# Moving one PSUM copy ahead of two normalising passes in a hand-ordered graph kernel

## The chip, the cores and the metric

The kernel runs on one core of a Trainium2 chip. The metric is the device time of one execution in microseconds, as the median of several runs. The engines are called PE (matrix engine; PEld is its loading of weights), DVE (vector), ACT (scalar, activations), POOL (GpSimd) and SP (which issues most DMAs).

## The reference

The input is a batch of 128 graphs of 128 nodes with 512 features, in fp32. Two layers follow each other, each on a normalised copy of the features (layernorm, then ReLU) with a residual connection.

```python
# layer 0: attention with 8 heads, scores multiplied by twice the adjacency
h = relu(layernorm(x))
q, k, v = h @ Wq.T + bq, h @ Wk.T + bk, h @ Wv.T + bv
scores = (q @ k.T) / sqrt(64) * (adj + adj)
x = x + (softmax(scores) @ v) @ Wo.T + bo
# layer 1: graph attention
h = relu(layernorm(x))
Wh = h @ W
e = leaky_relu(Wh @ a[:512] + (Wh @ a[512:]).T, 0.2)
att = softmax(where(adj > 0.5, e, -9e15), axis=1)   # over the rows
x = x + elu(att @ Wh)
```

## The kernel before

The kernel treats the batch as 64 pairs p of two graphs. The work on a pair is cut into small named steps (functions that issue a few instructions), and three lists give the order in which steps of different pairs are issued: HEAD at the start, ORDER for each round of the middle, TAIL at the end. Each engine then executes its own instructions in the order of issue. In ORDER a step is written `name:lag`, and round p issues it for the pair p - lag. So a round works on several pairs at once: in round p the scores of layer 0 belong to pair p, the contexts to pair p - 1, the normalising of layer 1 to pair p - 2 and the gather of layer 1 to pair p - 3.

The steps that matter here:

```python
    # all PSUM tiles come from one pool of eight
    ps1 = ctx.enter_context(tc.tile_pool(name="ps1", bufs=8, space=bass.MemoryType.PSUM))

    def row_stats(src, name, soon=False):                 # cut
        def stats(i):                                     # st0, st1: DVE
            nc.vector.bn_stats(st, src[:, i, :])
            nc.vector.bn_aggr(mv[:, i, :], st)
        def power():                                      # pw: POOL, 1/sqrt(var + eps)
            if not soon:
                nc.gpsimd.tensor_scalar_add(mv[:, :, 1], mv[:, :, 1], EPS)
            nc.gpsimd.tensor_tensor(mv[:, :, 1], mv[:, :, 1], mhalf.to_broadcast([P, 2]), OP.pow)

    def centre1(p):                                       # nm: DVE
        nc.vector.scalar_tensor_tensor(nmr, mv[:, :, 0], -1.0, mv[:, :, 1], op0=OP.mult, op1=OP.mult)

    def hidden1(p, i):                                    # h20, h21: ACT, normalising of batch i
        nc.scalar.activation(
            h1s[p][0][:, i, :], xs[p][:, i, :], AF.Relu, bias=nmr[:, i : i + 1], scale=mv[:, i, 1:2]
        )

    def dot1(p, i, k):                                    # d00 ... d11: DVE, reads what h20, h21 wrote
        ...

    def gather1(p, i):                                    # g0, g1: PE, the gather of batch i
        pg = ps1.tile([P, C, S], F32, name="pg", tag="ps1")
        for c in range(C):
            nc.tensor.matmul(pg[:, c, :], h1s[p][0][:, i, c * P : (c + 1) * P], wts[p][:, i, :], start=True, stop=True)
        pgs[p, i] = pg

    def keep_gathered(p, i):                              # ge0, ge1: ACT, copy of the gathered rows
        if p not in gTs:
            gTs[p] = work.tile([P, 7, 2, S], F32, name="gT")
        nc.scalar.copy(rows_of(gTs[p], i), pgs.pop((p, i)))

    def scores(b):                                        # sca, scb: PE, two PSUM tiles each
        ...
    def weigh(b, k):                                      # ata0, ata1, atb0, atb1: DVE, scores times adjacency
        ...                                               # then mxa (DVE), exa0-3 (ACT), fla (DVE)
    def context(b):                                       # pca, pcb: PE, one PSUM tile each
        pc = ps1.tile([P, C, S], F32, name="pc", tag="ps1")
        for j in range(C):
            for s in range(2):
                nc.tensor.matmul(pc[s * D : (s + 1) * D, j, :], vs[b // G][...], aT[:, :, s * C + j, :], start=True, stop=True)
    def keep_context(b):                                  # pea, peb: ACT
        nc.scalar.copy(rows_of(cxT, b % 2), pcs.pop(b))
```

The other names of ORDER that the text speaks of: U1 to U11 are the products for q, k and v (acc_a, acc_b, acc_c), F their copies by ACT, A their additions by DVE; o and w are the output products of the two layers (row_a, row_c). The first line of ORDER, which opens a round, is before

```
        U1:0 fa:4 ge0:3 pw:2 hs1:1 fb:4 g1:3 nm:2 lT:0 so:4 sca:0 h20:2 scb:0 h21:2 ata0:0 ge1:3 ata1:0 pca:1 mxa:0
        pcb:1 pea:1 d00:2 F1:0 U11:1 exa1:0 ...          # cut
```

The middle has the rounds p = 3 to 59. Odd and even rounds differ in which of the U products they issue.

Of the kernel before, what the change touches and what calls it, by code (L numbers as in the profile page):

```python
# [24 lines left out]
def kernel(  # L25
# [548 lines left out]
    def listed(text, mark):  # L574
# [24 lines left out]
        od6@1 od5@1 m1@0 e1@0 U7@2 A9@2 sw@0 st1@1 g0@0 F7@2 st0@1 F10@2 Ww3@0 A2@2 hd1@2  # L599
    """  # L600
    ORDER = """
        U1:0 fa:4 ge0:3 pw:2 hs1:1 fb:4 g1:3 nm:2 lT:0 so:4 sca:0 h20:2 scb:0 h21:2 ata0:0 ge1:3 ata1:0 pca:1 mxa:0
        pcb:1 pea:1 d00:2 F1:0 U11:1 exa1:0 A6:1 A8:1 U2:0 exa0:0 d10:2 exa3:0 t0:0 px:2 exa2:0 gs0:3 rca0:0 w0:3 pd:2
        A11:1 A10:8 A1:8 nma1:0 rca1:0 w1:3 gs1:3 t1:0 nma2:0 gs2:3 o0:1 s0:0 zc0:3 nma0:0 lx:1 wd1:3 U3:0 nma3:0 hs3:1
        d01:2 fla:0 o1:1 F3:0 peb:1 w2:3 atb0:0 bla:0 atb1:0 w3:3 zc2:3 mxb:0 F2:0 la:-1 w4:3 pv:2 gs3:3 lt:2 U5:0 zc4:3
# [223 lines left out]
```

## Time and profile before

| | |
|---|---|
| time, median of 3 runs | 2364.43 us (2360.34 to 2364.67) |
| span of the profiled run | 2362.5 us |
| mean granted TensorE clock | 0.997 |
| copy gT, ACT, 128 x 512, 128 times | 576 ns median |
| normalising pass h, ACT, 128 x 512, 128 times | 812 ns median |
| DMA traffic | 314.06 MB, mean 133 GB/s |

A busy line of the profile has an engine, its busy time in us, its share of the span and its instructions. A line of the timeline has the start in us from the start of the span, the length of the merged group, engine, line of the kernel, operation, output and inputs with shapes, the number of instructions, and in brackets how long the engine had been idle and what released it. A wait that is put down to one engine is the one of several that ended last.

### The profile page before, as it was taken

The numbers are of one execution on the slowest core, as the hardware profiler recorded it, in microseconds if no ns is written. First come the engines' busy times: TensorE is split into PE (matmuls) and PEld (weight loads), VectorE is DVE, ScalarE is ACT, GpSimd is POOL, SyncE is SP. The second block draws the span as 40 slices with busy tenths as digits, with TensorE's granted clock in tenths as the row PEclk, the third lists the DMA queues.
The fourth block names the chain that finished last, engine by engine and source line by source line (L and its number), as shares of the span: only waits on it lengthen the run. The fifth ranks groups of instructions, "written<-read, shape, count | busy, mean of one in ns | idle before, by whom it ended". The sixth has DMA issues, their size and how long they took to land.

```text
span 2362.5 us, 41114 instructions
## 1 busy us (share of the span) xinstructions
PE 2337.6 (99%) x14184; PEld 2066.2 (87%) x14184; DVE 2002.0 (85%) x4113; ACT 1458.1 (62%) x4815; POOL 256.9 (11%) x320
## 2 busy tenths in 40 slices
PE   9999999999999999999999999999999999999998
PEld 8888888888888888888888888888888888888886
DVE  5888888888888888888888888888888888888888
ACT  2656666666566665666666666656666565666775
POOL 1101101111101011011110111110101101110000
PEclk8999999999999999999999999999999999999999
DMA  4444353454444544444535345444454443443332
GB/s 156 140 115 148 123 152 114 127 157 127 140 131 125 149 131 135 139 114 143 148 124 152 117 123 159 125 142 126 130 147 132 134 139 113 145 147 119 117 119 94
DMA packets 267353, 314.06 MB, mean 133 GB/s; under 512 B 24201, under 2 KB 192137, under 8 KB 267145
## 3 DMA queue, kind: packets, MB, share of 16 engines
q1 hardware_dynamic: 263112, 311.31, 43.5%
q8 instruction: 112, 1.84, 0.3%
q0 software_dynamic: 1920, 0.13, 0.2%
q14 instruction: 97, 0.79, 0.1%
q10 hardware_dynamic: 2112, 0.01, 0.1%
HBM read 210.51 MB, written 100.85 MB: 132 GB/s over the span
## 4 chain that ended last, share of the span: by engine, by line
PE 89%; DVE 4%; POOL 3%; ACT 3%; issue 1%; DMA 0%; POOLq 0%; ACTq 0%; SPq 0%; DVEq 0%
PE acc_a L258 26%; PE row_a L299 23%; PE acc_c L258 12%; PE row_c L299 8%; PE acc_b L258 7%; PE pc L388 5%; PE sc L320 3%; PE pg L481 3%; POOL mv L173 2%; ACT h L418 2%; DVE st L165 2%; POOL mv L172 1%; DVE x L402 1%; DVE v L279 1%; ACT gT L487 1%
## 5 line engine op out<-in xcount | busy, mean ns | idle before, releaser
L339 ACT ACTIVATE at<-at,nmx 128x128 f32<-128x128 f32 x1024 | 396.2, 391 | 18.0 <-DVE nmx L334 17.9
L299 PE MATMUL row_a<-wo,cxT 128*128 128x256 f32 x1280 | 328.5, 379 | 0.3 <-DVE cxT L153 0.3
L348 ACT ACTIVATE at<-at,rs 128x128 f32<-128x128 f32 x1024 | 323.8, 392 | 4.3 <-DVE rs L343 4.1
L299 PE MATMUL row_a<-w,gT 128*128 128x256 f32 x1280 | 319.4, 380 | 2.9 <-DVE z L499 1.7
L172 POOL TENSOR_SCALAR mv<-mv 128x2 f32<-128x2 f32 x124 | 79.1, 638 | 2033.0 <-DVE mv L166 2010.8
L299 PEld LDWEIGHTS row_a<-w,gT 128*128 128x128 f32 x1280 | 242.3, 190 | 37.9 <-DVE z L499 2.6
L299 PEld LDWEIGHTS row_a<-wo,cxT 128*128 128x128 f32 x1280 | 242.6, 190 | 34.3 <-DVE cxT L153 0.6
L402 DVE TENSOR_TENSOR x<-row_a,x 128x256 f32<-128x256 f32 x320 | 135.2, 422 | 146.6 <-PE row_a L299 143.8
L495 ACT COPY z<-row_a 128x256 f32<-128x256 f32 x256 | 94.6, 369 | 210.2 <-PE row_a L299 210.0
L275 ACT ACTIVATE kT<-acc_a,bk 128x256 f32<-128x256 f32 x256 | 106.7, 467 | 178.4 <-PE acc_a L258 175.2
L327 DVE SCALAR_TENSOR_TENSOR at<-sc,adj 128x512 f32<-128x512 f32 x256 | 165.1, 686 | 42.2 <-PE sc L320 39.8
L339 ACT ACTIVATION_READ_ACCUMULATOR at<-at,nmx 128x1 f32 x1024 | 194.4, 190 | 0.0
L418 ACT ACTIVATE h<-x,nmr,mv 128x512 f32<-128x512 f32 x128 | 97.5, 807 | 151.2 <-DVE nmr L412 148.9
L165 DVE BATCH_NORM_STATS2 st<-x 128x6 f32<-128x512 f32 x256 | 176.3, 689 | 7.4 <-DMA x<-in_x 5.0
L275 ACT ACTIVATE qT<-acc_a,bq 128x256 f32<-128x256 f32 x256 | 106.3, 467 | 123.1 <-PE acc_a L258 123.1
L425 DVE SCALAR_TENSOR_TENSOR junk<-h,u 128x512 f32<-128x512 f32 x256 | 173.5, 678 | 0.6
L355 DVE STREAM_TRANSPOSE tr<-at 128x1024 f32<-128x1024 f32 x128 | 158.9, 1241 | 7.0 <-PE pc L388 2.7
L334 DVE TENSOR_REDUCE nmx<-at 128x8 f32<-128x1024 f32 x128 | 156.2, 1220 | 4.3
L481 PEld LDWEIGHTS pg<-w,h 128*128 128x128 f32 x1024 | 133.3, 192 | 6.6 <-ACT z L495 0.2
L388 PE MATMUL pc<-aT,v 128*64 128x128 f32 x2048 | 127.6, 277 | 11.1 <-ACT gT L487 11.0
L173 POOL TENSOR_TENSOR mv<-mv,mhalf 128x2 f32<-128x2 f32 x128 | 131.0, 1024 | 30.9 <-DVE mv L168 20.6
L481 PE MATMUL pg<-w,h 128*128 128x128 f32 x1024 | 134.1, 275 | 0.0
(130 smaller groups left out, 4868.0 us busy)
## 6 DMA issues: line engine op xcount, KB each, us to landing
blocks<-tr SPq DMA_DIRECT2D x128, 512.0 KB, 6.5
aT<-blocks SPq DMA_DIRECT2D x512, 128.0 KB, 2.9
x<-in_x SPq DMA_DIRECT2D x123, 512.0 KB, 5.1
out<-x SPq DMA_DIRECT2D x63, 512.0 KB, 4.1
hA<-in_xT SPq DMA_DIRECT2D x120, 256.0 KB, 3.6
mr<-rows SPq DMA_DIRECT2D x60, 256.0 KB, 4.1
adj<-in_adj SPq DMA_DIRECT2D x64, 128.0 KB, 4.1
adjT<-in_adjT SPq DMA_DIRECT2D x64, 128.0 KB, 3.7
```

Source lines behind the costliest of these rows:

```text
L165: nc.vector.bn_stats(st, src[:, i, :])
L173: nc.gpsimd.tensor_tensor(mv[:, :, 1], mv[:, :, 1], mhalf.to_broadcast([P, 2]), OP.pow)
L258: nc.tensor.matmul(acc[:, m, :], lhsT, rhs, start=fresh and m == 0 and c == 0, stop=c == 1, skip_group_check=True)
L275: nc.scalar.activation(dst(t, f)[:, m, :], a[:, m, :], AF.Identity, bias=bias[:, j : j + 1])
L299: nc.tensor.matmul(acc, left[:, la, c, :], w[:, wb, c, :], start=n in (0, 3) and c == 0, stop=c == 1, skip_group_check=True)
L327: nc.vector.scalar_tensor_tensor(ats[b][0][:, k * C : (k + 1) * C, :], scs[b][k], QSCALE, adjs[p][:, i : i + 1, :].to_broadcast([P, C, S]) ...
L339: nc.scalar.activation(at[:, j, :], at[:, j, :], AF.Exp, bias=nmx[:, j : j + 1], accum_out=sums[:, j : j + 1])
L348: nc.scalar.activation(at[:, j, :], at[:, j, :], AF.Copy, scale=rs[:, j : j + 1])
L355: nc.vector.transpose(trs[b], at.rearrange("p h (j k) -> p j h k", k=Q))
L388: nc.tensor.matmul(pc[s * D : (s + 1) * D, j, :], vs[b // G][:, b % G, head * D : (head + 1) * D], aT[:, :, s * C + j, :], start=True, sto ...
L425: nc.vector.scalar_tensor_tensor(junk, h2[:, i, :], 1.0, u_sb[:, k, :], op0=OP.mult, op1=OP.mult, accum_out=ws[:, i, 1:2] if k else src_sb ...
L481: nc.tensor.matmul(pg[:, c, :], h1s[p][0][:, i, c * P : (c + 1) * P], wts[p][:, i, :], start=True, stop=True)
```

## The change

In ORDER the step ge1 moves from behind h21 and ata0 to the place ahead of h20. ACT thus copies the second gathered tile of pair p - 3 before it normalises the two batches of pair p - 2. Nothing else moves; HEAD and TAIL stay as they are. It is meant to free the PSUM tile of the second gather without waiting for the statistics that the normalising needs.

```diff
     ORDER = """
-        U1:0 fa:4 ge0:3 pw:2 hs1:1 fb:4 g1:3 nm:2 lT:0 so:4 sca:0 h20:2 scb:0 h21:2 ata0:0 ge1:3 ata1:0 pca:1 mxa:0
+        U1:0 fa:4 ge0:3 pw:2 hs1:1 fb:4 g1:3 nm:2 lT:0 so:4 sca:0 ge1:3 h20:2 scb:0 h21:2 ata0:0 ata1:0 pca:1 mxa:0
         pcb:1 pea:1 d00:2 F1:0 U11:1 exa1:0 A6:1 A8:1 U2:0 exa0:0 d10:2 exa3:0 t0:0 px:2 exa2:0 gs0:3 rca0:0 w0:3 pd:2
```

## The prediction

> **What bounds the kernel now.** I read the shares of busy time first, then who waited for whom, then the chain of waits around one instance of the longest wait of the matrix engine (PE), and last the timeline of two neighbouring rounds of the middle.
>
> ```profile
> PE 2337.6 (99%) x14184; PEld 2066.2 (87%) x14184; DVE 2002.0 (85%) x4113; ACT 1458.1 (62%) x4815; POOL 256.9 (11%) x320
> ```
>
> PE is busy for 2337.6 of 2362.5 us. Only about 25 us are idle, and that is nearly all that a change of order alone could bring back. From the view of waits:
>
> ```profile
> ACT h L418 <- DVE nmr L412: 148.9, 60, 3.1
> ...
> PEld pc L388 <- ACT gT L487: 16.6, 29, 0.6
> ...
> PE pc L388 <- ACT gT L487: 11.0, 28, 0.4
> ```
>
> The columns are total us, times, longest. ACT waits some 2.5 us per round before it normalises (148.9 / 60), which costs nothing by itself. But PE waits in turn for a copy that ACT makes after it: the context products (pc) wait for the copy of gathered rows (gT), 0.4 us, 28 times, 11.0 us. No other wait of PE exceeds 2.7 us in the whole run. The chain of waits from 1080 to 1090 us says how that wait comes about (start, us, what):
>
> ```profile
> 1082.37 1.02 POOL mv L172
> ...
> 1083.47 1.76 POOL mv L173
> ...
> 1085.25 0.17 DVE nmr L412
> ...
> 1085.51 1.52 ACT h L418 x2
> 1087.03 0.48 ACT gT L487
> 1087.51 0.04 issue
> 1087.55 1.97 PE pc L388 x32
> ```
>
> The statistics go through two slow POOL operations, then nmr on DVE, then two normalising passes on ACT (h20, h21), and only then comes the copy ge1, though it needs nothing of all that. PE stands behind it. The timeline of an odd round:
>
> ```profile
> 1084.12 1.05 PE L481 MATMUL pg<-w,h 128*128 128x128 f32 x8
> ...
> 1085.10 2.06 PE L320 MATMUL sc<-kT,qT 64*128 64x128 f32 x32
> ...
> 1085.51 1.52 ACT L418 ACTIVATE h<-x,nmr,mv 128x512 f32<-128x512 f32 x2 [2.34 <-DVE nmr L412]
> ...
> 1086.94 0.56 ACT L487 COPY gT<-pg 128x512 f32<-128x512 f32 x1
> ...
> 1087.55 1.97 PE L388 MATMUL pc<-aT,v 128*64 128x128 f32 x32 [0.40 <-ACT gT L487]
> ...
> 1088.69 0.59 ACT L395 COPY cxT<-pc 128x512 f32<-128x512 f32 x1 [1.19 <-PE pc L388]
> ...
> 1089.45 1.99 PE L258 MATMUL acc_a<-hS,wq 128*128 128x256 f32 x8
> ```
>
> and of the even round after it:
>
> ```profile
> 1120.79 2.06 PE L320 MATMUL sc<-kT,qT 64*128 64x128 f32 x32
> ...
> 1121.66 1.52 ACT L418 ACTIVATE h<-x,nmr,mv 128x512 f32<-128x512 f32 x2 [2.80 <-DVE nmr L412]
> ...
> 1122.77 2.02 PE L388 MATMUL pc<-aT,v 128*64 128x128 f32 x32
> 1123.08 0.57 ACT L487 COPY gT<-pg 128x512 f32<-128x512 f32 x1
> ...
> 1124.72 1.99 PE L258 MATMUL acc_c<-hA,wk 128*128 128x256 f32 x8
> ```
>
> Here pc starts before the gT copy, without a gap. The two kinds of round differ in which PSUM tile the first context takes: in the odd rounds of the built program it is the buffer that the second pg has just left, so the first context product (pca) waits for ge1. In the even rounds it is the second (pcb), 16 matmuls or 0.93 us later, and at 1123.70 it finds ge1 done (1123.08 + 0.57 = 1123.65).
>
> **What the Trainium skill says.** "Perfetto Trace Analysis", section "Tensor Engine Instruction (MATMUL, LD_WEIGHTS)": ACT works off its queue strictly first in, first out, so a ready copy behind an unready pass waits with it; the trace agrees, since the pg that ge1 reads has its last matmul end at 1085.17 (1084.12 + 1.05), ACT idles 2.34 us until 1085.51, and the copy still starts at 1086.94. The same section says that the profiler's matmul ends are modelled; so I take PE's delays below from starts, not from ends. "PSUM — Partial Sum Buffer", section "Specifications (TRN2)": eight banks of 512 fp32 values a partition; each tile pg, sc, pc (4 x 128 fp32) fills one, so a new tile waits for the last reader of an old one, as pc does here. "Perfetto Trace Analysis", section "Optimization Strategy": the same gap repeating on the engine that should be saturated can mean too few buffers; the trace has that gap every second round (pc starts at 1014.88, 1087.55, 1160.24, period 72.67 us for two rounds).
>
> **The change part by part.**
> Nothing is added or removed. In each of the 57 rounds of the middle (p = 3 to 59) one ACT instruction, the copy ge1, stands before two others. PE, DVE, POOL and the DMA queues keep their order. The buffers of PSUM are handed out so that odd rounds keep the relation pca after ge1; in even rounds the two contexts swap, so that pca follows ge1 and pcb the first scores tile.
>
> *Odd rounds, PE.* Without a wait the context starts 1.98 us after the scores (even round: 1122.77 - 1120.79). With it, 2.45 us (1087.55 - 1085.10): 0.47 us late. The next product follows 1.90 us after the start of the context here (1089.45 - 1087.55) and 1.95 in the even round (1124.72 - 1122.77), so 0.05 of the delay is made up. A round loses 0.42 us. After the change ge1 starts where ACT is idle anyway, at about 1085.2 when pg is done, and ends near 1085.8, which is 1.3 us before pca can start (1085.10 + 1.98 = 1087.08). So the whole 0.42 goes.
>
> *How many.* The odd rounds 3 to 59 are 29. 27 of them, at 215.57 to 2104.88 us, lose 0.42: 11.34 us. The first (pc at 142.90, scores at 140.56) loses 2.34 - 1.98 - 0.05 = 0.31, the last (2177.24 and 2175.10) 2.14 - 1.98 - 0.05 = 0.11. Sum 11.8 us.
>
> *Even rounds.* No PE wait today, so no gain. After the change pca waits for ge1, which ends near 1121.5 (pg is done at about 1120.9, ACT idle) against a start at 1122.77; pcb at 1123.70 waits for the weighing of the scores, done by 1122.7. Zero.
>
> *ACT, odd rounds.* The normalising pass starts when the copy leaves ACT rather than at 1085.51: an ACT pass of this size holds its successor back by about 0.5 us (1088.69 to 1089.18), so 1085.2 + 0.5 = 1085.7, about 0.2 to 0.3 us late. h20 then ends near 1086.6 and its reader, the dot product on DVE, starts at 1088.75. h21's reader comes later still. Hidden.
>
> 2364.4 - 11.8 = 2352.6 us.
>
> **The rivals.**
> *A second wait takes over.* PE becomes 0.42 us earlier against the others. The tightest place I find behind the stall is a row_c product whose PSUM tile is the scores tile that DVE weighs. The timeline has
>
> ```profile
> 1096.28 1.29 DVE L327 SCALAR_TENSOR_TENSOR at<-sc,adj 128x512 f32<-128x512 f32 x2
> ...
> 1097.33 1.03 PE L299 MATMUL row_c<-w,gT 128*128 128x256 f32 x4
> ```
>
> The first of the two weighings ends at 1096.97, 0.35 us before the product, and PE would now be there at 1096.91. If DVE kept its time, 0.06 us plus some 0.1 us of signalling (as from nmr's end at 1085.41 to h at 1085.51) would be lost, and the gain would be about 0.26 x 29 = 7.5 us: 2357. Against it: DVE hangs on PE there. Its flip before the weighing waits for ACT's exponentials, and these for the context copy, which itself waits 1.19 us for pc. With pc 0.42 earlier the exponentials can start at about 1088.9 (the row maximum ends at 1088.83) in place of 1089.18, so this chain moves up by some 0.25 us, and 0.2 us of margin stay. I hold this for possible, not likely.
> *The later normalising is paid somewhere.* If the 0.2 to 0.3 us of h20 reached PE through the dot products, the score row's trip through memory and the gather of the next round, it would eat most of the gain: 2358 to 2362. Against it: the gather in the next round starts 4.0 us after DVE has finished its weights (timeline: 1113.17 against 1117.18), so that is covered several times over.
> *The wait was only a sign of something else*, as the arrival of aT by DMA. Then nothing changes: 2364. Against it: in the even rounds the same loads are there in time, and the gap follows the end of gT by 0.05 us each time.
> *ACT serving ge1 early makes ACT late.* ACT is 62% busy and idle for 2.3 to 2.8 us just there; I see no way.
>
> **Range and chances.** Full gain 2352.6; with the second wait 2357; nothing 2364. The three times before differ by 4.3 us (2360.34 to 2364.67), which is a third of the gain, and the after times may sit at either side. I take 2349 to 2358 for 8 in 10. The gain is 0.5%; even removing all 25 us of PE idle would be 1.1%, so faster by over 2% is excluded but for surprise (0.01), and slower by 2% (47 us) would need a new wait of 0.8 us in each of 57 rounds, which no slack shows (0.01).
>
> **What would show it.** In the profile after: the wait of PE's pc for gT gone (0 of 28); ACT's wait before h shorter and split, with some of it before gT; pc to scores 1.98 us in odd rounds too; two rounds in 72.25 us in place of 72.67; PE busy unchanged near 2337 us and the span shorter by 12. It would be wrong if a new PE wait of 0.1 us or more appears about 29 times (row_c on the weighing first of all), or if the round takes 72.67 us without the gap, which would mean that PE's pace there is set elsewhere.

## The result, and the profile after

| | before | after |
|---|---|---|
| time, median of 4 runs each | 2362.39 us (2360.27 to 2364.67) | 2350.05 us (2347.95 to 2352.19) |
| ratio after / before, 95% interval | | 0.9948 (0.9930 to 0.9965) |

The kernel is 12.3 us faster (half a per cent); predicted were 11.8. (The 2352.6 us predicted count from the 2364.4 of three runs; over four runs the kernel before takes 2362.4.) The spans of the two profiles differ by more, 16.4 us (2362.5 and 2346.1). To see how much of that is the change, cut both at the first scores of the middle and at the scores of its last round. This is the view of stretches of time: from and to, length, busy time of PE, PEld, DVE, ACT and POOL with their instructions, granted clock of PE, share of DMA and GB/s. Before:

```profile
0.00:140.50 140.50, 135.71 (x756) 118.86 (x756) 103.51 (x206) 66.29 (x217) 16.98 (x28) 0.95 0.49 149
140.50:2175.00 2034.50, 2023.51 (x12322) 1794.30 (x12320) 1737.35 (x3558) 1269.67 (x4200) 232.19 (x280) 1.00 0.45 134
2175.00:2362.50 187.50, 178.42 (x1110) 153.04 (x1108) 161.15 (x351) 122.16 (x398) 7.73 (x12) 0.99 0.35 109
```

After:

```profile
0.00:136.90 136.90, 131.72 (x756) 115.63 (x756) 103.51 (x206) 66.23 (x217) 16.99 (x28) 0.98 0.50 153
136.90:2158.90 2022.00, 2022.00 (x12322) 1792.58 (x12322) 1735.84 (x3558) 1278.76 (x4200) 232.27 (x280) 1.00 0.46 135
2158.90:2346.10 187.20, 178.25 (x1109) 152.98 (x1108) 161.07 (x350) 122.22 (x398) 7.74 (x12) 1.00 0.35 110
```

The middle gives 12.5 us, and there PE is now busy for the whole stretch: 2022.00 of 2022.00 us, against 2023.51 of 2034.50. (A full row doesn't mean that nothing is left; w4_first, below, takes 1.4 us more off it.) The end gives 0.3. The start gives 3.6 us, but the two kernels are the same there: the same 756 matmuls took 4.0 us less, at a granted clock of 0.98 in place of 0.95. That doesn't belong to the change (last section).

Who waited for whom, after:

```profile
ACT gT L487 <- PE pg L481: 117.4, 59, 2.0
...
ACT h L418 <- DVE nmr L412: 6.0, 4, 3.1
...
PEld row_c L299 <- DVE at L327: 5.2, 28, 0.2
```

PE's wait of pc for gT (11.0 us, 28 times) is gone. ACT's long wait has moved: it stands ahead of the gT copy now, for the gather's products, and hardly any is left ahead of h. The last line is new: PE's loading of weights for a row_c product waits 0.19 us for the weighing on DVE, 28 times, in odd rounds. The timeline of an odd round after:

```profile
1075.70 2.06 PE L320 MATMUL sc<-kT,qT 64*128 64x128 f32 x32
1075.81 0.58 ACT L487 COPY gT<-pg 128x512 f32<-128x512 f32 x1 [2.03 <-PE pg L481]
...
1076.29 1.52 ACT L418 ACTIVATE h<-x,nmr,mv 128x512 f32<-128x512 f32 x2
...
1077.68 1.97 PE L388 MATMUL pc<-aT,v 128*64 128x128 f32 x32
...
1078.83 0.58 ACT L395 COPY cxT<-pc 128x512 f32<-128x512 f32 x1 [1.02 <-PE pc L388]
...
1079.47 0.40 ACT L339 ACTIVATE at<-at,nmx 128x128 f32<-128x128 f32 x1
```

The contexts start 1.98 us after the scores (before: 2.45), and the copy ends 1.3 us ahead of them. For all of what follows I read such distances from the starts of matmuls in the trace, as means over 25 odd and 25 even rounds (p = 5 to 54):

| us | scores to pca | pca to pcb | pcb to next product | odd round | scores to pca | pca to pcb | pcb to next product | even round |
|---|---|---|---|---|---|---|---|---|
| before | 2.452 | 0.924 | 0.973 | 35.684 | 1.985 | 0.924 | 1.011 | 36.982 |
| after | 1.985 | 0.924 | 0.973 | 35.268 | 1.985 | 0.924 | 0.973 | 36.944 |

(The four columns left are of odd rounds, the four right of even ones.) The odd round became 0.416 us shorter and the even one 0.038. The context of an odd round starts 0.467 us sooner, so 0.05 of it is given back later in the round; and the even rounds had held pcb for 0.04 us without any gap on the page. The odd and even rounds together make up the gain of the middle: 28 x (0.416 + 0.038) = 12.7 us, against the 12.5 above.

### The profile page after: what moved, and what is told of

Same layout as the page of the kernel before. It is cut to its first block, busy times and chain, and to the rows that moved or that the text cites. A ratio compares the mean times of both kernels' runs of the same rounds, so it can differ in the third digit from the quotient of the medians.

```text
span 2346.1 us, 41028 instructions
## 1 busy us (share of the span) xinstructions
PE 2332.0 (99%) x14184; PEld 2061.2 (88%) x14184; DVE 2000.4 (85%) x4113; ACT 1467.2 (63%) x4815; POOL 257.0 (11%) x320
## 4 chain that ended last, share of the span: by engine, by line
PE 99%; DVE 0%; ACT 0%; DMA 0%; issue 0%; POOL 0%; SPq 0%; ACTq 0%; DVEq 0%; POOLq 0%
PE acc_a L258 29%; PE row_a L299 24%; PE acc_c L258 14%; PE row_c L299 9%; PE acc_b L258 7%; PE sc L320 5%; PE pc L388 5%; PE pg L481 5%; PE pt L197 0%; DMA x<-in_x 0%; PE pm L531 0%; DVE st L165 0%; ACT z L495 0%; PE pu L553 0%; DVE z L499 0%
## 5 line engine op out<-in xcount | busy, mean ns | idle before, releaser
L487 ACT COPY gT<-pg 128x512 f32<-128x512 f32 x128 | 74.6, 584 | 123.8 <-PE pg L481 117.4
L299 PE MATMUL row_c<-w,gT 128*128 128x256 f32 x512 | 133.0, 382 | 0.6 <-DVE z L499 0.5
```

The source lines that it names most:

```text
L299: nc.tensor.matmul(acc, left[:, la, c, :], w[:, wb, c, :], start=n in (0, 3) and c == 0, stop=c == 1, skip_group_check=True)
```

## The experiments

The rival to my theory (a PSUM tile that is emptied late holds the first context of odd rounds) was that the copy, or ACT's work in general, holds PE up in another way. In the table "middle" is from the first scores of the middle to those of its last round, 56 rounds, which keeps start and end out. The ratios are taken against runs of the kernel before that were made alongside, with medians from 2362.4 to 2365.4 us; the middle is of one profile each, and tells the runs apart more finely.

| run | time, us | ratio to before (95%) | odd round | even round | middle |
|---|---|---|---|---|---|
| before | | | 35.684 | 36.982 | 2034.5 |
| after | 2350.1 | 0.9948 (0.9930 to 0.9965) | 35.268 | 36.944 | 2022.0 |
| odd | 2351.8 | 0.9955 (0.9940 to 0.9969) | 35.269 | 36.982 | 2023.3 |
| even | 2363.9 | 1.0002 (0.9993 to 1.0011) | 35.683 | 36.944 | 2033.5 |
| twice_late | 2357.8 | 0.9975 (0.9968 to 0.9982) | 35.428 | 36.944 | 2026.3 |
| twice_early | 2352.9 | 0.9955 (0.9939 to 0.9971) | 35.270 | 36.944 | 2022.0 |
| soon | 2369.5 | 1.0025 (1.0018 to 1.0032) | 35.402 | 37.397 | 2038.8 |
| between | 2357.4 | 0.9976 (0.9969 to 0.9984) | 35.267 | 37.146 | 2027.6 |
| norm_twice | 2351.1 | 0.9949 (0.9934 to 0.9964) | 35.217 | 36.944 | 2020.5 |
| w4_first | 2350.0 | 0.9942 (0.9925 to 0.9959) | 35.217 | 36.944 | 2020.5 |
| norm_skip | 2350.3 | 0.9934 (0.9917 to 0.9950) | 35.217 | 36.944 | 2020.5 |

**odd and even: half the change each.** The order of the change in rounds of one parity only.

```diff
+        at = ORDER.index(("h20", 2))
+        early = [s for s in ORDER if s != ("ge1", 3)]
+        early.insert(at, ("ge1", 3))
         for p in range(EARLY, N - LATE):
-            for step, lag in ORDER:
+            for step, lag in (early if p % 2 == 1 else ORDER):     # even: p % 2 == 0
```

> The copy ge1 stands ahead of the normalising in odd rounds only. My theory (the first context of an odd round waits for the PSUM tile that ge1 empties): the context starts 1.98 us after the scores in odd rounds, in place of 2.45, and the odd round is 0.42 us shorter; even rounds keep their 36.98 us. Time some 11.5 us below the kernel before. The rival, that the gain is spread over all rounds because ACT is simply better packed: half the gain, about 6 us, and the odd round shorter by 0.2 only.

> The copy ge1 stands ahead of the normalising in even rounds only. As predicted (no wait of PE there, so no gain): no change of time, even rounds 36.98 us as before, the odd rounds keep the gap of 0.40 us. The trace after the change suggests a little more: the second context of an even round was held by 0.04 us although no gap shows, so the even round would be 0.04 us shorter, 1.1 us in all. The rival of better packed ACT: about 6 us less.

The odd half brings the odd rounds the whole 0.415 us and leaves the even ones alone; the even half brings 0.038 us an even round. In the middle that is 11.3 and 1.1 us of 12.6. The 1.1 us are read from the rounds alone; the times can't show them (ratio 1.0002, 0.9993 to 1.0011). So the gain isn't spread over ACT's work: it sits in the rounds in which pca takes the tile of ge1 in the old order too. In the run of the even half PE's wait stays as it was:

```profile
PE pc L388 <- ACT gT L487: 11.0, 28, 0.4
```

**twice_late: more work, just as late, but another buffer.** The old order, with the copy made twice.

```diff
-        nc.scalar.copy(rows_of(gTs[p], i), pgs.pop((p, i)))
+        for _ in range(1 + i):
+            nc.scalar.copy(rows_of(gTs[p], i), pgs[p, i])
+        pgs.pop((p, i))
```

> The copy ge1 keeps its old, late place and is made twice, so that ACT has 64 copies more to do and the gathered rows are ready some 0.5 us later than before. The buffers of PSUM are handed out anew for this: the first context of an odd round now takes the tile of the first scores, the second the tile that ge1 empties. My theory (it is the buffer of the first context, not the lateness of the copy): the first context starts 1.98 us after the scores, the second is held by 0.05 to 0.1 us, and the kernel is about 10 us faster than before although ACT does more and does it later. The rival (the late copy itself, or its readers, hold PE up): each round 0.4 to 0.5 us longer, 2385 us or more.

ACT does more and finishes later, and yet the kernel is faster: 0.9975. Scores to pca is 1.985 us in odd rounds, since pca has another tile. Now pcb is held: pca to pcb 1.084 in place of 0.924, and 0.05 more up to the next product. That is 0.21 us an odd round and not the 0.05 to 0.1 I expected, so the middle gained 8.3 us, and the time 6, in place of 10. The view of waits of this run shows it on the weights alone, as 0.2 us each:

```profile
PEld pc L388 <- ACT gT L488: 6.2, 27, 0.2
```

In even rounds of this run neither context takes the tile of ge1 but a product behind them does, and there the late copy costs nothing: 36.944 us. What costs is which product stands behind the tile. This also answers the rival that aT comes late by DMA: with another tile, pca of the odd rounds starts at 1.985 us.

**twice_early: the changed order with the copy made twice.** The same edit on the changed kernel.

> The changed kernel (ge1 ahead of the normalising in all rounds of the middle) with ge1 made twice. In the changed kernel the first context starts 1.29 us after the end of ge1, so another 0.5 us fits in: my theory expects the time of the changed kernel within 1 us, some 12 us below the kernel before, with h 0.5 us later and no new wait of PE. The rival, that the later normalising is paid for downstream: 0.5 us in each of 57 rounds, up to 28 us more.

Rounds of 35.270 and 36.944 us, as after, and the same 2022.0 us for the middle; the time is 2.8 us above that of the changed kernel, with intervals of the ratio that overlap. The normalising starts 1.21 us after the scores in odd rounds (after: 0.59), and this is paid for nowhere in the middle.

**between: the copy between the two passes.**

```diff
-        ... sca:0 h20:2 scb:0 h21:2 ata0:0 ge1:3 ata1:0 pca:1 mxa:0
+        ... sca:0 h20:2 scb:0 ge1:3 h21:2 ata0:0 ata1:0 pca:1 mxa:0
```

> The copy ge1 stands between the two normalising passes h20 and h21. My theory, by the clock of one round each: in odd rounds ge1 ends about 0.7 us earlier than before, in time, so the full 0.42 us is gained; in even rounds the first context now takes the tile that ge1 empties, and ge1 ends one pass (0.72 us) after the start of the normalising, 0.2 us later than the context could start: scores to context 2.2 us in place of 1.98, and the even round 0.2 us longer. In all 6 to 7 us faster than the kernel before. The rival, that ge1 needs only to leave the last place: 12 us faster as with the change.

The odd rounds gain all (35.267), the even ones lose 0.16 against before (37.146): scores to pca 2.187 us there, 0.20 over the free distance, as worked out. An even round of this run in the timeline:

```profile
1117.47 2.06 PE L320 MATMUL sc<-kT,qT 64*128 64x128 f32 x32
1118.33 0.81 ACT L418 ACTIVATE h<-x,nmr,mv 128x512 f32<-128x512 f32 x1 [2.79 <-DVE nmr L412]
1119.05 0.56 ACT L487 COPY gT<-pg 128x512 f32<-128x512 f32 x1
...
1119.67 1.73 PEld L388 LDWEIGHTS pc<-aT,v 128*64 128x64 f32 x32 [0.34 <-ACT gT L487]
1119.67 1.97 PE L388 MATMUL pc<-aT,v 128*64 128x128 f32 x32
```

The copy ends at 1119.61, pc starts at 1119.67. Note how little of this delay of 0.20 us the page tells: PE's row is empty for 0.14 us only (the modelled end of the scores is 1119.53), and no wait is named there, but on the weights alone. In twice_late a delay of 0.16 us left no gap on PE's row at all. Half a step earlier is thus not enough: the new order gives the tile of ge1 to pca in even rounds too, and only the place ahead of both passes serves both.

**soon: make the statistics faster instead.** The old order; the addition of epsilon goes from POOL to DVE.

```diff
-            l1s[p] = row_stats(xs[p], "mv1")
+            l1s[p] = row_stats(xs[p], "mv1", soon=True)
```

> The order of steps is the old one, with ge1 behind the normalising; but the addition of epsilon to the variance of layer 1 goes from POOL (one of the two POOL operations on the way to the normalising, 1.02 us) to DVE as two one-column additions. My theory (ge1 is late only because the normalising ahead of it waits for the statistics): nmr comes some 0.7 us earlier, ge1 ends before the context needs its tile, the scores to context distance of odd rounds falls from 2.45 to 1.98 us, and the kernel takes 2352 us as with the change, 12 us below the kernel before. The rival, that the place of ge1 behind two passes of 0.7 us is enough to hold PE: gap of 0.3 to 0.4 us stays in odd rounds, no gain.

This expectation failed: the kernel is slower. In odd rounds the gap shrinks, scores to pca 2.169 us, but in even rounds a new one opens, pca to pcb 1.327 us. An even round of this run:

```profile
1118.12 1.22 DVE L515 SCALAR_TENSOR_TENSOR x<-ez,x 128x1024 f32<-128x1024 f32 x1
...
1118.23 2.06 PE L320 MATMUL sc<-kT,qT 64*128 64x128 f32 x32
1119.25 0.15 DVE L412 SCALAR_TENSOR_TENSOR nmr<-mv 128x2 f32<-128x2 f32 x1
...
1119.49 1.52 ACT L418 ACTIVATE h<-x,nmr,mv 128x512 f32<-128x512 f32 x2 [3.20 <-PE sc L320]
...
1120.92 0.56 ACT L487 COPY gT<-pg 128x512 f32<-128x512 f32 x1
...
1121.54 1.09 PE L388 MATMUL pc<-aT,v 128*64 128x128 f32 x16 [0.23 <-ACT gT L487]
```

DVE makes nmr right behind the second finishing pass (L515), without a wait, so DVE's own row sets its time, and the two added instructions make that row longer. (The wait of h is put down to the scores; what h reads is nmr, which ends at 1119.40, 0.09 us before h starts.) In even rounds it was so before:

```profile
1120.27 1.22 DVE L515 SCALAR_TENSOR_TENSOR x<-ez,x 128x1024 f32<-128x1024 f32 x1
1121.41 0.15 DVE L412 SCALAR_TENSOR_TENSOR nmr<-mv 128x2 f32<-128x2 f32 x1
```

There POOL had ended at 1120.93, 0.48 us ahead of nmr; only in odd rounds did nmr follow POOL. I had counted POOL's leg as the chain of both and left DVE's order out. The run still speaks for the theory, by size: relative to the scores, h starts 0.28 us sooner in odd rounds (0.13 us after them, before 0.41), and pca comes 0.28 sooner; in even rounds nmr and h start 0.42 us later (h 1.27, before 0.85), and pcb comes 0.40 later. PE follows the copy one to one. In every round type in which a context is clearly held, it starts 0.05 us after the copy ends, wherever that is: in us from the scores, copy and context at 2.40 and 2.45 (before, odd), 2.13 and 2.19 (between, even), 2.12 and 2.17 (soon, odd), 3.26 and 3.31 (soon, even), 3.02 and 3.07 (twice_late, odd).

**norm_twice, norm_skip and w4_first: the 0.05 us given back.** All on the changed kernel. In its odd rounds row_c takes the tile of the second graph's scores (scb). DVE weighs them (atb0) behind the flip (fla, its transpose of the first graph's attention), and the flip waits for ACT's exponentials and the eight passes that divide the attention by its sums. After the change:

```profile
1086.66 1.29 DVE L327 SCALAR_TENSOR_TENSOR at<-sc,adj 128x512 f32<-128x512 f32 x2
...
1087.40 0.73 PEld L299 LDWEIGHTS row_c<-w,gT 128*128 128x128 f32 x4 [0.19 <-DVE at L327]
1087.46 1.08 PE L299 MATMUL row_c<-w,gT 128*128 128x256 f32 x4
```

```diff
         for j in range(2 * k, 2 * k + 2):
             nc.scalar.activation(at[:, j, :], at[:, j, :], AF.Copy, scale=rs[:, j : j + 1])
+        if k == 3 and b % 2 == 0:                                  # norm_twice: head 7 divided twice
+            nc.scalar.activation(at[:, j, :], at[:, j, :], AF.Copy, scale=rs[:, j : j + 1])
```

> The changed kernel, with one of the eight passes that divide the attention of the first graph of a pair by its sums made twice (so one head of it is divided twice, and the output is not the reference's). It tests the wait that the change uncovers: in odd rounds the product row_c stands 0.05 us longer, because its tile is the scores tile that DVE weighs after the flip, and the flip waits for the last of these passes. If that chain bounds PE now, another pass of 0.29 us makes the odd round about 0.3 us longer (35.57 us) and leaves the even round at 36.94: 8 to 9 us slower than the changed kernel. If the 0.05 us are something else, nothing changes, since ACT is idle for a third of the time.

No such thing came: 35.217 us, shorter than after. The built program explains it. The buffers of PSUM are handed out when the kernel is built, and with the pass added row_c got the tile of a context copy and acc_b, two products later, that of the scores. So this run doesn't lengthen the wait, it removes it. A run with the tile kept was needed:

```diff
-        for j in range(2 * k, 2 * k + 2):
+        for j in range(2 * k, 2 * k + (1 if k == 3 and b % 2 == 0 else 2)):   # norm_skip: head 7 left undivided
```

> The changed kernel, with one of the eight passes that divide the attention of the first graph of a pair by its sums left out (one head of it stays undivided, so the output is not the reference's). In the run in which a pass was doubled, the buffers of PSUM had been handed out differently: row_c took the tile of a context copy, and its wait was gone. Here row_c keeps the tile of the scores as in the changed kernel, and the chain of exponentials, normalising passes, flip and weighing is one pass shorter, 0.2 to 0.3 us. If that chain holds row_c, its wait in odd rounds goes and the odd round takes 35.22 us in place of 35.27, the even one 36.94 as before; 1.4 us below the changed kernel. If something else does, row_c keeps its 0.19 us wait for weights in 28 rounds.

Met: row_c has the same tile as after, the chain is a pass shorter, the line of its wait is gone from the waits, and the odd round is 35.217 us. The third way leaves the work whole and has PE do another product first:

```diff
-        d01:2 fla:0 o1:1 F3:0 peb:1 w2:3 atb0:0 bla:0 atb1:0 w3:3 zc2:3 mxb:0 F2:0 la:-1 w4:3 pv:2 gs3:3 ...
+        d01:2 fla:0 w2:3 F3:0 o1:1 zc2:3 peb:1 atb0:0 bla:0 atb1:0 w4:3 w3:3 mxb:0 F2:0 la:-1 pv:2 gs3:3 ...
```

> The changed kernel, with PE's products in another order so that the row_c product stands 0.86 us later: w2, o1, w4, w3 in place of o1, w2, w3, w4, and the copy zc2 ahead of the context copy peb. If the chain through the weighing is what holds row_c, its wait goes: the odd round is 0.05 us shorter (35.22 us), the even round 36.94, 1.5 us below the changed kernel. The risk is a new wait of w4 for zc2 or of the next product for peb; then the rounds are longer by what shows there.

35.217 us as expected, and the middle takes 2020.5 us, 14.0 below before and 1.4 below after. It leaves no work out and is the shortest such version by its rounds; its time of 2350.0 us can't be told from that of the changed kernel (intervals 0.9925 to 0.9959 and 0.9930 to 0.9965).

## Why the prediction was right, and where it wasn't

- *The wait and its cause.* Right. The gap came from the normalising ahead of ge1, and PE stood behind the tile; odd, twice_late and between show each part. ACT waits for pg in place of nmr, as said.
- *The size in odd rounds.* 0.42 predicted, 0.416 measured, but that agreement is luck: the parts were wrong and made up for each other. I took 0.05 us off the delay of 0.47, because the stretch from pca to the next product looked shorter in the odd round than in the even. It wasn't made up: the even round was the long one, since its pcb was held by 0.04 us. The whole 0.467 was to be had, and 0.05 was lost to row_c.
- *Even rounds: "Zero".* Wrong by a small term: 0.038 us each, 1.1 us in all (run even). The sign was there, pcb's start 0.05 us behind the end of the copy, the same distance as at the visible gap. I read it as just in time.
- *The second wait.* I named the right place and judged it "not likely", with 0.2 us of margin. The chain through the exponentials did move up, by 0.22 us at the end of the weighing (11.87 us after the scores before, 11.65 after) in place of 0.25. But I measured the margin at the start of the product. Its weights load 0.21 us ahead of that where nothing holds them (norm_skip, 11.54 and 11.76 us after the scores), and they wait as well: 0.19 us on the weights, 0.05 on the round. By the letter of my own sign of being wrong (a new wait of 0.1 us or more, about 29 times, row_c first of all) it came; its cost did not. The 7.5 us of that rival would have needed DVE to stay where it was.
- *The later normalising.* In odd rounds h started 0.18 us later against the scores (0.59, before 0.41), predicted 0.2 to 0.3, and twice_early shows that even half a microsecond more stays hidden.
- *The pace.* 72.25 us for two rounds predicted, 72.21 measured. PE's busy time, predicted unchanged, is 5.6 us lower: 4.0 of that in the start, where the clock differed, and 1.5 in the middle, probably because the modelled ends of held matmuls count as work. The idle time of PE, too, isn't the ceiling that I took it for: in the middle the page shows 11.0 us of it before, and w4_first takes 14.0 us less.

## What to carry to other kernels

When an engine at 99% shows the same small gap every second round, ask which buffer the held instruction takes and what stands ahead of the work that frees it. A copy that empties PSUM belongs ahead of passes that wait for something else, if its own input comes sooner than theirs. Take the slack of a product from the load of its weights and from starts of instructions, since a product that is held by 0.04 to 0.16 us showed no gap here; and look at what buffers each variant is given, for an edit elsewhere can move them.

## What the hardware showed beyond that

The start of the program came in two lengths, whatever the kernel: the first scores of the middle lie at 136.0 to 137.2 us in four of the eleven profiles and at 140.2 to 140.9 us in seven. The granted clock of PE over that stretch was 0.98 or 0.99 in all four short ones and 0.95 or 0.96 in all seven long ones. This is about the spread of 4 us between runs of one kernel, a third of the gain here: the four times of the kernel before are two near 2360.3 and two near 2364.6 us, those of the changed one two near 2348.0 and two near 2352.1, so like against like, if the pairs are the two lengths, the gain is 12.3 and 12.5 us. The profile before has a long start and the one after a short one, which is why they differ by 16.4. The end of the program varied too, from 187.2 to 189.8 us over the eleven profiles; the cause of that stays open. The Trainium skill, "TensorE: Matmul & The Clock Gate", section "Part 1: The HAM clock gate (the "warmup" mystery)", says that the time a program starts at the reduced clock varies from run to run, by where the activity window of the clock gate stands; the two lengths and their clocks agree with that in kind, but no run here shows that it is the cause.
